# A state-space layer with a mixture of experts on one core: who writes the taps, where the imaginary parts land, how the sums are read back, and the order of the steps

## The chip, the core and the metric

The kernel runs on one core of a Trainium2 chip. The core has a matrix engine (TensorE, in the profile PE, with its weight loads apart as PEld), a vector engine (VectorE, DVE), a scalar engine (ScalarE, ACT), a general engine (GpSimd, POOL) and a queue engine (SyncE, SP), and 16 DMA engines that move data between device memory and the on-chip memories: SBUF (128 partitions) and PSUM, into which PE writes. Each engine works through its own instructions in order and waits on semaphores for the others. SP and ACT can both issue plain DMAs; POOL issues the indirect ones (scatters by a list of rows).

The metric is the device time of one execution in microseconds. Before the change: 341.56 us, the median of three runs (341.54 to 342.92).

## What is computed

All in float32, for x of shape (2, 2048, 128). It is a layer norm, a diagonal state-space layer (S4D) with a gated linear unit and two residuals, then a second layer norm and a mixture of 14 routed experts (the best two of each token) and 2 shared ones. Cut to what matters:

```python
# first half, x2 = layernorm(x)
u  = swapaxes(x2 @ in_W.T + in_b, 1, 2)
dt = exp(log_dt);  A = -exp(log_A_real) + 1j * A_imag;  dtA = A * dt[:, None]
K  = exp(dtA[:, :, None] * arange(L))
k  = 2 * einsum('hn,hnl->hl', Cc * (exp(dtA) - 1) / A, K).real
y  = causal_convolution(u, k) + u * D_skip[:, None]        # by FFT in the reference
z  = einsum('oh,bhl->bol', glu_W, gelu(y)) + glu_b
a, g = split(z);  x = x + (swap(a * sigmoid(g)) @ out_W.T + out_b + x2)
# second half, xf = layernorm(x) as 4096 rows
gates = softmax(xf @ router_w);  the two best, made to sum to 1
expert(e) = silu((xf * rsqrt(mean(xf**2)) * rms[e]) @ W1[e]) @ W2[e]
x = x + sum over the two best of gate * expert(e) + both shared experts
```

## The kernel before

**Modes and powers.** The 4096 complex modes are laid out as 128 partitions by 32. DVE computes A (line 272: the real part from an exponential, the imaginary part by a copy of the tile `aim`, line 274, which SP loaded, line 129), then the powers Z and, by doubling, PW (`double`). While it does so, X (the input, 32 blocks of 128 tokens) arrives in eight loads, the even ones issued by SP, the odd ones by ACT (line 134); PE turns the blocks and ACT copies them into XT, which shares its memory with the later tile Y.

**Taps and Toeplitz tiles.** For each of four groups g, `taps(g)` has PE multiply powers into a PSUM tile, ACT copy four strips of it into the tile `kk`, and SP write `kk` to a table in device memory, `kp` (line 403). `toeplitz(n)` for n = 2g and 2g + 1 then has SP load shifted views of that table, four loads each (line 418): those are the Toeplitz matrices with which PE convolves inside a chunk of 128 tokens (`inside`). Those of n = 5 and 6 go into XT's memory (shown as Y<-kp). `turned(g)` has PE turn the powers and ACT copy them to VT, for the sums over a chunk (`chunk_sums`). DVE combines chunk sums into states (`turns`, `scan`), PE applies them (yps<-PW,ST, in two halves of 256 matmuls), ACT takes the gelu, DVE transposes into Y.

An engine wrapped in `Ordered` (line 94) keeps its instructions in the order in which the program names them: ACT, PE and POOL from line 228, DVE from line 353, SP from the step early2; all but POOL are released after the last tile. Elsewhere the framework's scheduler orders them.

**Units, shared experts and steps.** The tokens are 8 blocks of 512. `Unit` u0 to u4 take blocks 0, 1-2, 3-4, 5-6 and 7 through the gated unit, the projection, the residual, the layer norm, the router and the choice of two experts. Its steps by engine: gate, value, project, turn, logits, count on PE; tanh, biased, rows, turned, copies, exps on ACT; gated, add, scales, unscale, choose, slots on DVE; scatter on POOL, which writes each token's row twice, to the places of its two experts in the table `xs_rows`, 8 scatters for u0 and u4, 16 for each other. `Shared` s0 to s5 do the two shared experts for one block: first (PE), silu (ACT), second (PE), add (DVE). A "scale" multiplies one expert's weights by its norm weights (ACT). early1, early2, table1 and table2 make the table of the experts' tiles. `STEPS` (line 50) is one list of 226 such steps, written out by hand; each engine takes its own from it in that order.

**Tiles.** 77 tiles of 128 rows: SP (and for odd late tiles ACT) loads the rows xg, SP copies the expert's first weights wg within SBUF, PE turns the rows and multiplies twice, ACT applies silu, DVE scales by the gate (yo), POOL scatters 128 result rows to the table `res` by the goal that travelled with each row (`goal`, line 702: 2 x 4096 rows, row 256k + 2p + a for block k, partition p and choice a).

**The tail.** `summands(j)` loads the two results of each of a block's 512 tokens (1155, all on SP, in pieces of 1 KB); `finish(j, rd)` adds the two (1160), adds X (1161) and stores (1163, SP, in pieces of 512 bytes). The shared experts of the last two blocks (LATE = 2) run here, s6 and s7; their `add` (1131) puts the PSUM tile pz into X first.

Of the kernel before, what the change touches and what calls it, by code (L numbers as in the profile page):

```python
# [18 lines left out]
P = 128  # L19
# [28 lines left out]


STEPS = """  # L50
u0.parts.0 u1.gate.0 u1.value.0 u1.biased.0 u0.gated.0 u0.project.0 u1.gate.1 u1.tanh.0
u1.value.1 u0.add.0 u1.tanh.1 u1.gated.0 u1.biased.1 u1.project.0 u0.scales u2.gate.0
u2.tanh.0 u1.gated.1 u2.gate.1 u1.project.1 u1.add.0 u2.value.1 u0.rows.0 u2.tanh.1
u2.value.0 u1.add.1 u0.turn.0 u0.unscale u0.turned.0 u2.biased.0 u2.biased.1 u0.logits.0
u0.copies.0 u1.scales u1.rows.0 u1.rows.1 u3.gate.0 u3.gate.1 u2.gated.0 u1.turn.0 u0.choose
u2.gated.1 u1.turned.0 u0.exps u2.project.0 u1.turn.1 u3.tanh.0 scale u1.turned.1 scale
scale u0.count u3.tanh.1 u2.add.0 u3.value.0 u1.logits.0 u1.logits.1 u0.slots u0.scatter
u1.copies.1 u3.biased.0 u1.unscale u2.project.1 u1.choose u3.gated.0 u1.exps s0.first.0
s0.first.1 s0.silu.0 u3.value.1 u1.count scale s0.silu.1 s0.first.2 s0.first.3 u3.project.0
u2.add.1 u1.copies.0 u1.slots u1.scatter s0.second.0 scale s0.second.1 u2.scales s0.silu.2  # L60
scale scale u3.biased.1 u3.gated.1 u2.rows.0 u3.add.0 u3.project.1 u2.turn.0 s0.second.2
u2.rows.1 u3.add.1 u2.turn.1 u2.unscale u2.turned.0 scale s0.silu.3 u2.turned.1 u3.scales
u2.copies.0 u2.logits.0 u2.copies.1 u2.logits.1 s0.second.3 scale u3.rows.0 u2.choose
s1.first.0 u3.rows.1 u3.turn.0 s1.first.1 s1.first.2 u2.count u3.turned.0 s1.silu.0 u2.exps
u2.slots u2.scatter u3.turn.1 s1.silu.1 u3.turned.1 u3.logits.0 u3.copies.0 s1.first.3
s1.silu.3 s1.second.0 u4.gate.0 s1.silu.2 u4.tanh.0 s0.add u3.logits.1 s1.second.1
s1.second.2 u3.unscale s1.second.3 u3.copies.1 u4.value.0 u3.choose u4.biased.0 u3.exps
s2.first.0 s2.first.1 u4.gated.0 s2.silu.0 s2.first.2 s1.add u4.project.0 s2.second.0
s2.silu.1 u4.add.0 u3.count s2.second.1 u4.scales u3.slots u3.scatter s2.silu.2 scale
s2.first.3 s2.silu.3 s2.second.2 s2.second.3 s3.first.0 scale s3.first.1 scale scale  # L70
s3.silu.0 s3.second.0 s3.first.2 s3.silu.1 u4.rows.0 s3.second.1 s3.silu.2 u4.turn.0
s3.first.3 u4.unscale u4.turned.0 s3.second.2 s3.silu.3 s3.second.3 s4.first.0 u4.logits.0
scale s4.first.1 scale early1 s2.add u4.choose s4.first.2 s4.silu.0 s4.second.0 s4.silu.1
s3.add u4.copies.0 s4.first.3 s4.second.1 u4.count scale s4.silu.2 s4.second.2 s4.silu.3
u4.exps s4.second.3 early2 s5.first.0 s5.first.1 s5.silu.0 s5.first.2 s5.second.0 u4.slots
u4.scatter table1 s5.silu.2 s5.silu.1 s5.first.3 s5.silu.3 s5.second.1 s5.second.2
s5.second.3 s5.add table2 s4.add
"""


# [27 lines left out]
def s4d_glu_moe_kernel(  # L108
# [112 lines left out]
    with ExitStack() as ssm:  # L221
# [160 lines left out]
        def taps(g):  # L382

            kps = pss.tile([P, P], F32, name=f"kps_{g}", tag="ps")
            for i in range(2):
                for c in range(2):
                    for a in range(4):
                        q = 8 * g + 4 * i + a
                        T.matmul(
                            kps[a * NM:a * NM + 8, :], lhsT=BC[:, c, q, :], rhs=PW[:, c, q, 0:P],  # L390
                            start=(i == 0 and c == 0), stop=False, skip_group_check=True,
                        )
            for a in range(4):
# [9 lines left out]
            Q.dma_start(out=kp, in_=kk)  # L403
            kpd[g] = kp

        def toeplitz(g):
# [691 lines left out]
    class Shared:  # L1098
# [29 lines left out]

        def add(self):
            xf = X[:, self.j * TB:(self.j + 1) * TB, :].rearrange("p k d -> p (k d)")  # L1130
            V.tensor_tensor(xf, self.pz, xf, ALU.add)

        def whole(self):
# [174 lines left out]
```

## Time and profile before

The profiled execution took 342.49 us; its span, from the first to the last instruction, is 340.8 us, and all times below count from the span's start.

| engine | busy us | share of span | instructions |
|---|---|---|---|
| PE | 267.3 | 78% | 2951 |
| PEld | 222.8 | 65% | 2951 |
| DVE | 225.3 | 66% | 787 |
| ACT | 169.6 | 50% | 434 |
| POOL | 149.5 | 44% | 249 |

| part of the execution | from, to (us) |
|---|---|
| modes, powers, states (DVE, then PE) | 4.4, 103.8 |
| gelu and transposes | 103.8, 109.5 |
| units and shared experts in the order of the list | 106.3, 207 |
| row scatters on POOL | 136.6, 217.9 |
| result scatters on POOL | 218.2, 317.4 |
| loads of results, sums, stores | 318.8, 338.9 |

Reading it: a row of a view in order of time has the start, the duration (of all its instructions together), the engine, the line, the operation, the tensors written and read, a count, and in brackets the idle time before it with what ended it; "issue" stands for an idle time that the profile can't put down to anything. L102 is the line of the helper that records ordered instructions, so tiles are told apart by name. A q after an engine's name means the engine issuing a DMA; the DMA's data move later. A row of a view by stretches has the stretch, its length, the busy time and count of PE, PEld, DVE, ACT and POOL, PE's granted clock, the DMA engines' mean busy share, and GB/s. The busy share of an engine is a mean over stages: where POOL stands at 7 tenths, the rest is the pause of 0.30 us between two scatters.

### The profile page before, as it was taken

What the parts mean: (1) busy time and instruction counts of PE and PEld (TensorE: products, weight loads), DVE (VectorE), ACT (ScalarE), POOL (GpSimd) and SP (SyncE); (2) the same over time, 40 slices, a digit from 0 to 9 for tenths busy, and PEclk for the clock granted to TensorE, in tenths of its full rate; (3) what the DMA queues carried; (4) which work ended last, traced back from release to release, by engine and by line L of the source; (5) the groups of instructions that cost most, each with busy time, mean ns of one, the idle gap of its engine ahead of it and who ended that gap; (6) DMA issues with size and microseconds to landing.
All of it is one profiled execution on the core that took longest, in us unless ns stands there. A gap on an engine that the chain in (4) does not pass through costs nothing.

```text
span 340.8 us, 8883 instructions
## 1 busy us (share of the span) xinstructions
PE 267.3 (78%) x2951; PEld 222.8 (65%) x2951; DVE 225.3 (66%) x787; ACT 169.6 (50%) x434; POOL 149.5 (44%) x249
## 2 busy tenths in 40 slices
PE   1895868756796988979989973997988978889910
PEld 1885666445695446567767752987878878777710
DVE  4999889999965598897776362452554545453093
ACT  1699594597055589779677540331332322224300
POOL 5400000000001200777777777777777777777200
PEclk9999589998997898797999997797999999999985
DMA  8300181966700991111111155656666766651398
GB/s 217 87 4 0 49 213 33 240 156 178 197 4 3 281 298 28 46 49 56 55 49 55 57 171 150 184 164 205 185 187 190 210 216 194 201 160 30 126 348 264
DMA packets 66895, 47.19 MB, mean 138 GB/s; under 512 B 7304, under 2 KB 64782, under 8 KB 66850
## 3 DMA queue, kind: packets, MB, share of 16 engines
q1 hardware_dynamic: 55906, 35.11, 36.8%
q0 software_dynamic: 4512, 8.47, 7.6%
q10 hardware_dynamic: 6432, 3.05, 3.4%
q8 instruction: 24, 0.39, 0.5%
q14 instruction: 21, 0.17, 0.2%
HBM read 24.49 MB, written 12.86 MB: 110 GB/s over the span
## 4 chain that ended last, share of the span: by engine, by line
PE 41%; DVE 27%; DMA 14%; ACT 7%; issue 5%; SPq 2%; POOL 2%; DVEq 0%; ACTq 0%; POOLq 0%
PE pz L102 12%; PE ph L102 11%; DMA xg<-xs_rows 9%; DVE t L102 6%; PE yps L102 5%; DVE PW L102 3%; PE xgt L102 3%; DMA WB<-res 2%; DMA xs_rows<-pl,si 2%; ACT pl L102 2%; POOL xs_rows L102 2%; PE pa L102 2%; PE pg L102 1%; PE pr L102 1%; DVE U L102 1%
## 5 line engine op out<-in xcount | busy, mean ns | idle before, releaser
L102 POOL DMA_INDIRECT xs_rows<-pl,si x64 | 62.1, 970 | 42.6 <-ACT pl L102 23.4
L102 POOL DMA_INDIRECT res<-yo,to x65 | 64.0, 985 | 20.1 <-issue 9.1
L102 ACT ACTIVATE hs<-ph 128x256 f32<-128x256 f32 x77 | 29.4, 384 | 78.0 <-PE ph L102 48.6
L102 DVE TENSOR_SCALAR yo<-pz,xg 128x128 f32<-128x128 f32 x77 | 27.0, 351 | 40.9 <-PE pz L102 38.2
L102 PE MATMUL pz<-WB,hs 128*128 x308 | 49.9, 285 | 1.3 <-ACT hs L102 0.8
L102 PE MATMUL ph<-xgt,wg 128*128 128x128 f32 x308 | 49.5, 285 | 0.0
L102 PEld LDWEIGHTS pz<-WB,hs 128*128 128x128 f32 x308 | 41.8, 197 | 4.0 <-ACT hs L102 2.5
L102 PEld LDWEIGHTS ph<-xgt,wg 128*128 128x128 f32 x308 | 42.7, 201 | 0.3 <-DVE xgt L102 0.3
L102 POOL MEMSET blank<- 128x130 f32 x1 | 0.2, 208 | 93.3 <-DVE Y L102 93.3
L102 PE MATMUL xgt<-ident,xg 128*128 128x128 f32 x77 | 22.6, 295 | 16.1 <-DMA xg<-xs_rows 16.0
L102 DVE COPY xgt<-xgt 128x128 f32<-128x128 f32 x77 | 21.8, 283 | 16.2 <-PE xgt L102 15.3
L102 PEld LDWEIGHTS pz<-WB,hsh 128*128 128x128 f32 x192 | 24.0, 196 | 6.7 <-ACT hsh L102 3.3
L102 PE MATMUL ph<-XRT,WB 128*128 128x512 f32 x48 | 26.0, 657 | 1.5 <-DVE sv L102 1.5
L102 PE MATMUL pz<-WB,hsh 128*128 128x128 f32 x192 | 25.5, 284 | 1.6 <-ACT hsh L102 1.6
L102 ACT ACT_TABLE_LOAD x11 | 14.1, 1283 | 20.5 <-PE yps L102 11.9
L102 PEld LDWEIGHTS xgt<-ident,xg 128*128 128x128 f32 x77 | 11.3, 147 | 19.0 <-DMA xg<-xs_rows 18.8
L102 DVE TENSOR_TENSOR t<-PW,Z 128x512 f32<-128x512 f32 (+4 forms) x26 | 20.0, 809 | 0.4
L102 ACT ACTIVATE hsh<-ph 128x512 f32<-128x512 f32 x24 | 13.8, 597 | 9.4 <-PE ph L102 9.4
L102 PE MATMUL yps<-PW,ST 32*32 32x128 f32 x512 | 15.3, 268 | 3.5 <-issue 2.6
L102 PEld LDWEIGHTS yps<-PW,ST 32*32 32x32 f32 x512 | 13.9, 104 | 4.7 <-issue 3.5
L102 PE MATMUL pt<-flip,X 128*128 128x128 f32 x64 | 10.2, 315 | 7.4 <-DMA X<-in_x_dram 7.1
L102 ACT ACTIVATE pl<-X,mr,rq_y 128x128 f32<-128x128 f32 x32 | 12.8, 480 | 3.1 <-DVE mr L102 3.1
(244 smaller groups left out, 546.7 us busy)
## 6 DMA issues: line engine op xcount, KB each, us to landing
wg<-WB SPq DMA_DIRECT2D x77, 128.0 KB
toep<-kp SPq DMA_DIRECT2D x24, 256.0 KB
WB<-res SPq DMA_DIRECT2D x7, 512.0 KB
xg<-xs_rows SPq DMA_DIRECT2D x47, 65.0 KB
Y<-kp SPq DMA_DIRECT2D x8, 256.0 KB
xg<-xs_rows ACTq DMA_DIRECT2D x30, 65.0 KB
WB<-in_w_dram SPq DMA_DIRECT2D x2, 896.0 KB
WB<-in_w_dram SPq DMA_DIRECT2D x4, 448.0 KB
```

Of the source, the lines that this page charges most:

```text
L102: return self.tc.keep_in_program_order(getattr(self.engine, name)(*args, **kwargs))
```

## The change

It has five parts. The imaginary parts are loaded straight into A, which moves to a pool that lasts, by a DMA that ACT issues ahead of its X loads; DVE's copy goes. The taps are written to `kp` by a DMA that ACT issues after its copies, not SP. The rows of `res` are numbered so that the two results of a partition's four tokens of a block lie together: the loads have pieces of 4 KB, and both loads and stores alternate between SP (even blocks) and ACT (odd ones). s6 and s7 have no add in the tail any more: after the last product, PE multiplies X's block by the identity into the same PSUM tile, and `finish` reads that tile in X's place. The list of steps has the same 226 steps in another order.

```diff
-u0.parts.0 u1.gate.0 u1.value.0 u1.biased.0 u0.gated.0 u0.project.0 u1.gate.1 u1.tanh.0
-u1.value.1 u0.add.0 u1.tanh.1 u1.gated.0 u1.biased.1 u1.project.0 u0.scales u2.gate.0
-u2.tanh.0 u1.gated.1 u2.gate.1 u1.project.1 u1.add.0 u2.value.1 u0.rows.0 u2.tanh.1
-u2.value.0 u1.add.1 u0.turn.0 u0.unscale u0.turned.0 u2.biased.0 u2.biased.1 u0.logits.0
-u0.copies.0 u1.scales u1.rows.0 u1.rows.1 u3.gate.0 u3.gate.1 u2.gated.0 u1.turn.0 u0.choose
-u2.gated.1 u1.turned.0 u0.exps u2.project.0 u1.turn.1 u3.tanh.0 scale u1.turned.1 scale
-scale u0.count u3.tanh.1 u2.add.0 u3.value.0 u1.logits.0 u1.logits.1 u0.slots u0.scatter
-u1.copies.1 u3.biased.0 u1.unscale u2.project.1 u1.choose u3.gated.0 u1.exps s0.first.0
-s0.first.1 s0.silu.0 u3.value.1 u1.count scale s0.silu.1 s0.first.2 s0.first.3 u3.project.0
-u2.add.1 u1.copies.0 u1.slots u1.scatter s0.second.0 scale s0.second.1 u2.scales s0.silu.2
...
-s2.first.0 s2.first.1 u4.gated.0 s2.silu.0 s2.first.2 s1.add u4.project.0 s2.second.0
-s2.silu.1 u4.add.0 u3.count s2.second.1 u4.scales u3.slots u3.scatter s2.silu.2 scale
...
+u0.parts.0 u1.gate.0 u1.value.0 u0.gated.0 u0.project.0 u1.tanh.0 u1.gate.1 u0.add.0
+u1.value.1 u1.biased.0 u1.biased.1 u1.tanh.1 u2.gate.0 u1.gated.0 u1.project.0 u2.tanh.0
+u2.value.0 u0.scales u0.rows.0 u1.gated.1 u1.project.1 u2.gate.1 u1.add.0 u0.turn.0
+u2.value.1 u2.biased.0 u2.tanh.1 u3.gate.1 u0.unscale u0.turned.0 u1.add.1 u2.gated.0
+u0.copies.0 u0.logits.0 u1.scales u2.biased.1 u0.choose u1.rows.0 u2.project.0 u1.turn.0
+u1.rows.1 u0.exps u2.add.0 u1.copies.1 scale u3.gate.0 u0.count u0.slots u0.scatter
+u1.turned.0 scale u1.copies.0 u3.value.0 u1.turn.1 u1.unscale u1.turned.1 u2.gated.1 scale
+u1.logits.0 u1.logits.1 scale u2.project.1 u3.tanh.0 u3.biased.0 u1.choose u3.tanh.1 u1.exps
+u1.count u2.add.1 s0.first.0 s0.first.1 s0.silu.0 u1.slots u1.scatter u3.gated.0 s0.first.2
...
+s2.second.0 scale u3.choose s2.first.3 u4.gated.0 s2.silu.1 u4.project.0 scale s2.second.1
+s2.silu.2 s2.second.2 scale s1.add s2.silu.3 scale scale u3.exps s2.second.3 u3.count
+u4.add.0 u3.copies.0 u4.scales u3.slots s3.first.0 s2.add s3.first.1 s3.silu.0 u4.rows.0
+s3.first.2 s3.silu.1 s3.silu.2 u3.copies.1 u3.scatter early1 s3.first.3 s3.silu.3
...
-    aim = load("aim", a_im, [P, NQ])
+    A = const.tile([P, 2, NQ], F32, name="A")
+    S.dma_start(out=A[:, 1, :], in_=a_im)
...
-        A = tmp.tile([P, 2, NQ], F32, name="A")
         V.tensor_scalar(A[:, 0, :], ed[:, 0, :], -1.0, None, ALU.mult)
-        V.tensor_copy(A[:, 1, :], aim)
...
             kp = dram.tile([P, 2 * P], F32, name=f"kp_{g}")
-            Q.dma_start(out=kp, in_=kk)
+            S.dma_start(out=kp, in_=kk)
...
-    G.iota(goal, pattern=[[1, 2], [2 * P, NT]], base=0, channel_multiplier=2)
+    G.iota(
+        goal.rearrange("p a (j i) -> p a j i", i=TB),
+        pattern=[[1, 2], [2 * TB * P, NB], [2, TB]], base=0, channel_multiplier=2 * TB,
+    )
...
-        def second(self, n):
+        def residuals(self):
+            return X[:, self.j * TB:(self.j + 1) * TB, :].rearrange("p k d -> p (k d)")
+
+        def second(self, n, last=False):
...
-                    start=(n == 0 and k == 0), stop=(n == 3), skip_group_check=True,
+                    start=(n == 0 and k == 0), stop=(n == 3 and not last), skip_group_check=True,
                 )
+            if last:
+
+                T.matmul(
+                    self.pz, lhsT=ident, rhs=self.residuals(), start=False, stop=True,
+                    skip_group_check=True,
+                )
...
             for n in (2, 3):
-                self.second(n)
-            yield
-            self.add()
+                self.second(n, last=n == 3)
             yield
...
-        rd = rd.rearrange("p a b -> p (a b)").rearrange("p (i b) -> p i b", i=TB)
-        rv = res.rearrange("(i p a) d -> p i (a d)", a=2, p=P)
-        Q.dma_start(out=rd, in_=rv[:, j * TB:(j + 1) * TB, :])
-        return rd
-
-    def finish(j, rd):
+        rd = rd.rearrange("p a b -> p (a b)")
+        rv = res.rearrange("(j p r) d -> p j (r d)", r=2 * TB, p=P)
+        (S if j % 2 else Q).dma_start(out=rd, in_=rv[:, j])
+        return rd.rearrange("p (i b) -> p i b", i=TB)
+
+    def finish(j, rd, rest):
         ot = rd[:, :, :P]
         V.tensor_tensor(ot, ot, rd[:, :, P:], ALU.add)
-        V.tensor_tensor(ot, ot, X[:, j * TB:(j + 1) * TB, :], ALU.add)
+        V.tensor_tensor(ot, ot, rest, ALU.add)
         ov = out.rearrange("b (i p) d -> p (b i) d", p=P)
-        Q.dma_start(out=ov[:, j * TB:(j + 1) * TB, :], in_=ot)
+        (S if j % 2 else Q).dma_start(out=ov[:, j * TB:(j + 1) * TB, :], in_=ot)
...
-            finish(k, rds[k])
+            rest = X[:, k * TB:(k + 1) * TB, :]
+            if k >= NB - LATE:
+                rest = steps[f"s{k}"].pz.rearrange("p (i d) -> p i d", i=TB)
+            finish(k, rds[k], rest)
```

More of the change, by code (lines that the diff above doesn't have):

```diff
@@ L57 @@
-scale u0.count u3.tanh.1 u2.add.0 u3.value.0 u1.logits.0 u1.logits.1 u0.slots u0.scatter
-u1.copies.1 u3.biased.0 u1.unscale u2.project.1 u1.choose u3.gated.0 u1.exps s0.first.0
-s0.first.1 s0.silu.0 u3.value.1 u1.count scale s0.silu.1 s0.first.2 s0.first.3 u3.project.0
-u2.add.1 u1.copies.0 u1.slots u1.scatter s0.second.0 scale s0.second.1 u2.scales s0.silu.2
-scale scale u3.biased.1 u3.gated.1 u2.rows.0 u3.add.0 u3.project.1 u2.turn.0 s0.second.2
-u2.rows.1 u3.add.1 u2.turn.1 u2.unscale u2.turned.0 scale s0.silu.3 u2.turned.1 u3.scales
@@ L63 @@
[L63 to L67, printed above, removed]
-s2.first.0 s2.first.1 u4.gated.0 s2.silu.0 s2.first.2 s1.add u4.project.0 s2.second.0
@@ L69 @@
-s2.silu.1 u4.add.0 u3.count s2.second.1 u4.scales u3.slots u3.scatter s2.silu.2 scale
[L70 to L74, printed above, removed]
@@ L75 @@
-u4.exps s4.second.3 early2 s5.first.0 s5.first.1 s5.silu.0 s5.first.2 s5.second.0 u4.slots
-u4.scatter table1 s5.silu.2 s5.silu.1 s5.first.3 s5.silu.3 s5.second.1 s5.second.2
-s5.second.3 s5.add table2 s4.add
+u0.parts.0 u1.gate.0 u1.value.0 u0.gated.0 u0.project.0 u1.tanh.0 u1.gate.1 u0.add.0
+u1.value.1 u1.biased.0 u1.biased.1 u1.tanh.1 u2.gate.0 u1.gated.0 u1.project.0 u2.tanh.0
+u2.value.0 u0.scales u0.rows.0 u1.gated.1 u1.project.1 u2.gate.1 u1.add.0 u0.turn.0
+u2.value.1 u2.biased.0 u2.tanh.1 u3.gate.1 u0.unscale u0.turned.0 u1.add.1 u2.gated.0
@@ new lines @@
+u0.copies.0 u0.logits.0 u1.scales u2.biased.1 u0.choose u1.rows.0 u2.project.0 u1.turn.0
[3 more added lines that the diff above has]
+u1.count u2.add.1 s0.first.0 s0.first.1 s0.silu.0 u1.slots u1.scatter u3.gated.0 s0.first.2
+s0.silu.2 u3.value.1 s0.silu.1 u2.scales u3.biased.1 s0.second.0 u2.rows.0 s0.first.3
@@ new lines @@
+s0.silu.3 scale u3.gated.1 u3.project.0 u3.add.0 u3.project.1 u2.turn.0 u3.add.1 u2.rows.1
+s0.second.1 u2.turn.1 scale s0.second.2 u2.turned.0 scale u2.turned.1 u2.logits.0
+u2.logits.1 u2.copies.0 s0.second.3 u3.scales u3.rows.0 s1.first.0 s1.first.1 u2.unscale
+u3.turn.0 u3.rows.1 s1.silu.1 u2.choose s1.first.2 u2.count u3.turn.1 s1.silu.0 s1.second.0
+u2.exps s0.add u2.copies.1 u2.slots u2.scatter u3.turned.0 u4.gate.0 s1.silu.2 s1.second.1
+u3.logits.0 s1.first.3 s1.second.2 u3.turned.1 u3.unscale s1.silu.3 u4.value.0 s1.second.3
@@ new lines @@
+u3.logits.1 u4.tanh.0 u4.biased.0 s2.first.0 s2.silu.0 s2.first.1 scale s2.first.2
+s2.second.0 scale u3.choose s2.first.3 u4.gated.0 s2.silu.1 u4.project.0 scale s2.second.1
+s2.silu.2 s2.second.2 scale s1.add s2.silu.3 scale scale u3.exps s2.second.3 u3.count
+u4.add.0 u3.copies.0 u4.scales u3.slots s3.first.0 s2.add s3.first.1 s3.silu.0 u4.rows.0
+s3.first.2 s3.silu.1 s3.silu.2 u3.copies.1 u3.scatter early1 s3.first.3 s3.silu.3
+s3.second.0 u4.turn.0 u4.turned.0 u4.unscale s3.second.1 s3.second.2 s3.second.3 s3.add
@@ L78 @@
+s4.first.0 scale s4.silu.0 u4.logits.0 s4.first.1 scale scale s4.silu.1 u4.choose s4.first.2
+s4.silu.2 s4.second.0 s4.first.3 u4.count s4.second.1 s4.silu.3 u4.exps u4.copies.0 early2
+s4.second.2 s4.second.3 u4.slots u4.scatter s5.first.0 s5.silu.0 s5.first.1 s5.first.2
+s5.second.0 s5.silu.1 s5.second.1 s5.silu.2 s5.first.3 s5.silu.3 s5.second.2 table1 table2
+s5.second.3 s4.add s5.add
 """
@@ L1125, in second @@
                     self.pz[:, ks], lhsT=hs[:, ks], rhs=w[:, HID + f:HID + f + P],
-                    start=(n == 0 and k == 0), stop=(n == 3), skip_group_check=True,
+                    start=(n == 0 and k == 0), stop=(n == 3 and not last), skip_group_check=True,
[4 more added lines that the diff above has]
+                    skip_group_check=True,
                 )
         def add(self):
-            xf = X[:, self.j * TB:(self.j + 1) * TB, :].rearrange("p k d -> p (k d)")
+            xf = self.residuals()
             V.tensor_tensor(xf, self.pz, xf, ALU.add)
```

## The prediction

> **What bounds the kernel now.** I read the page's 40 slices first, then each engine in order of time, then short stretches.
>
> ```profile
> POOL 5400000000001200777777777777777777777200
> DMA  8300181966700991111111155656666766651398
> ...
> 136.60 1.19 POOL L102 DMA_INDIRECT xs_rows<-pl,si  x1 [23.44 <-ACT pl L102]
> 138.10 0.96 POOL L102 DMA_INDIRECT xs_rows<-pl,si  x1 [0.31 <-issue]
> ...
> 281.62 0.99 POOL L102 DMA_INDIRECT res<-yo,to  x1 [0.55 <-DVE yo L102]
> ...
> 316.43 0.98 POOL L102 DMA_INDIRECT res<-yo,to  x1 [0.30 <-issue]
> ```
>
> The first line is POOL's busy share by slice, a flat 7 through the middle. In order of time POOL issues 64 row scatters and 77 result scatters from 136.60 to 317.41, one each 1.27 or 1.29 us with 0.30 between; one pause, at 281.62, is longer (0.55). So the middle is one queue of 181 us. The chain of waits names PE and ACT there, but work that ends before POOL asks for it sets nothing. Two things count: when the first scatter starts, and whether POOL ever runs dry.
>
> Ahead of 136.60 the path is DVE from 4.38 to 84.55 (modes, powers, scans), then PE's end states, the gelu, and DVE and PE on unit u0.
>
> ```profile
> 64.55 0.69 SPq L403 DMA_DIRECT2D kp<-kk  x1
> 69.51 2.02 SPq L418 DMA_DIRECT2D toep<-kp  x4
> 71.57 5.17 SPq L418 DMA_DIRECT2D Y<-kp  x4
> 76.84 0.80 SPq L403 DMA_DIRECT2D kp<-kk  x1
> ...
> 88.44 3.70 PE L102 MATMUL yps<-PW,ST 32*32 32x128 f32 x128 [0.60 <-issue]
> 94.09 0.63 PE L102 MATMUL yps<-PW,ST 32*32 32x128 f32 x14 [1.96 <-issue]
> ...
> 96.54 1.71 PE L102 MATMUL yps<-PW,ST 32*32 32x128 f32 x53
> ```
>
> SP's queue: taps 2 left ScalarE at 62.05 and taps 3 at 67.88, but SP issues them at 64.55 and 76.84, being busy with the Toeplitz loads in between. PE: 0.60 and 1.96 us idle with no wait that the profile knows ("issue"), on the path, since DVE's states were there (84.55).
>
> The tail, by stretches of 1 us (DVE and ACT busy, clock, DMA share, GB/s in the last columns):
>
> ```profile
> 322.00:323.00 1.00, 1.00 (x12) 1.00 (x11) 0.00 (x0) 0.44 (x1) 0.00 (x0) 1.00 1.08 377
> 327.00:328.00 1.00, 0.00 (x0) 0.00 (x0) 1.00 (x2) 0.00 (x0) 0.00 (x0) 1.00 1.09 348
> 337.00:338.00 1.00, 0.00 (x0) 0.00 (x0) 0.00 (x0) 0.00 (x0) 0.00 (x0) 0.50 1.15 345
> ```
>
> From 321.0 to 338.9 the DMA engines never rest. DVE, also full from 323.02, ends at 335.04; the last stores still drain for 3.8 us. The transfers set the end.
>
> **The change, part by part.** Durations are from the profiled execution (span 340.8).
>
> *Imaginary parts in place.* The copy goes; it held DVE from 5.33 to 5.45, on the path: **−0.12**. The load (0.42 on SP) moves ahead of ACT's four X loads: those come 0.47 later, and ACT, which waits 3.41 us for PE before 9.18, covers that. SP's X loads and the thirteen small ones behind them come 0.47 earlier; PE starts at 7.10 on them, but DVE is the path, so 0. A is used first at 8.23, late enough for a load issued near 0.8 (prm, issued by 1.70, landed by 4.38).
>
> *Taps by ScalarE.* Four issues leave SP and enter ACT between the kk copies and the VT copies. An ACT issue of a similar load is 0.34 to 0.35 (xg), SP's of these taps 0.33 to 0.80. Behind it on ACT stand the VT copies, for which PE waits. g=0 is on the path: kk ends 38.06, issue to 38.45, VT copy 0.59 to 39.04; PE needs that PSUM buffer at 39.17, after its second batch. Covered by 0.13, so 0; at 0.80 it would cost 0.35. For g=1 to 3 DVE, full from 48 to 94.3, covers it.
>
> What it gives back: taps 2 start at 62.1, taps 3 at 67.9. SP now stands idle 4.27 before 69.51 and 3.96 before 81.60 until taps have landed; most of that goes. The Toeplitz traffic, which now ends at about 91.9 (stretches of 2 us: share 1.12 at 88 to 90, 0.01 at 92 to 94), would end near 85.5: 4.19 MB of g=4 to 7 from 68.3, where the share now drops to 0.28, at about 245 GB/s (206 to 298 from 84 to 92).
>
> Why that matters: PE's unexplained idles come after 127, 128 and 128 matmuls with weight loads (ended 82.64, 88.44, 94.09), and the page's queue called instruction has 24 packets of 16 KB. I read them as code arriving late behind data. Once the DMA is quiet, PE runs 256 from 96.54 to 103.80 without a stop. With the traffic gone by 86, the second idle goes; the code for the first is asked for while data still flow. Without the second, the later half's states start at 94.58, not 96.54; without both, at 94.32, since DVE's last states end at 94.28; so −2.22 is the cap. The other bound: denser traffic at 71 to 83 may lengthen the idle before 82.64 from 1.19 to the longest seen, 4.59; PE has 1.27 to spare there (83.28 against 84.55), so 2.1 late, less 1.96 saved: +0.1. I take **−1.96**, the idle whose cover of traffic is gone longest.
>
> [...]
>
> *Another step list.* It has the same 226 steps. Ahead of u0.slots, DVE has one step fewer: u2.gated.1 (130.80 in the old order).
>
> ```profile
> 130.80 0.68 DVE L102 SCALAR_TENSOR_TENSOR y<-th,av 128x512 f32<-128x512 f32 x1
> 131.40 0.68 DVE L102 TENSOR_TENSOR X<-po,X 128x512 f32<-128x512 f32 x1
> ...
> 133.19 0.27 DVE L102 TENSOR_TENSOR_SCAN run<-going,pm 128x70 f32<-128x70 f32 x1
> ...
> 135.49 0.17 DVE L102 COPY pl<-goal 128x8 int32<-128x8 int32 x1
> ```
>
> DVE is without a gap from 115.25 to 135.66, so the step's 0.60 comes off. PE and ACT keep up: in the new order u0's XRT copy ends near 124.2 and its logits near 125.6, two us before DVE's choose. **−0.60**. Bounds: 0, if another wait fills it; −1.4, if POOL's 0.94 between DVE's last write (135.66) and 136.60 was a wait for the ACT copy that ended 136.45, u1.copies.1, which now stands before u0.slots.
>
> Does POOL starve? The units' first scatters come at 146.95, 167.42, 187.81 and 208.04; the slots end at 145.98, 164.55, 180.59 and 198.92. POOL asks 0.6 earlier now. u1 loses the same DVE step and a 0.50 wait for PE: ready 144.9, due 146.3. u2 gains s0.add (0.6) after it lost 1.1: about 164, due 166.8. u3.count has four more matmul steps ahead (s2.first.3, s2.second.1 to 3, some 3.6 us): slots by 184.2, its second copy, now behind s3.silu.2, by about 185; due 187.2. u4 has four fewer. No stall: 0.
>
> *Tail.* Loads are 8 of 512 KB in 1 KB pieces, then in 4 KB; stores stay 8 of 256 KB in 512-byte pieces. Per engine of 16, a 512-byte piece took 23.7 ns (stores alone, 345.5 GB/s), a 1 KB piece 43.2 (loads alone, 379). That is 4.2 fixed and 19.5 per 512 bytes; so 160 for 4 KB, 409 GB/s. 4.19 MB in 10.25 instead of 11.07: **−0.82**. Bounds: 0, if pieces cost nothing; −2.4, where DVE takes over. The two additions of 0.60 that leave DVE do not show while transfers set the end. DVE ends by 334.3: first pair landing near 323.6, then 16 operations of 0.668 (12.02 for 18 now). With 0.63 to issue and 1.8 to land (taps: 38.13 to 39.95) that is 336.5 at the earliest. Two queues save issue time, which no one awaits. PE gets 2 x 0.86 for the residual product, from 325.4 to 327.1, before the sixth and seventh sums at 331.6. Behind ACT's four loads may stand eight silu of 0.52; held to 320.9, PE would end near 333 and DVE by 335, still ahead of the transfers.
>
> Sum: 0.12 + 1.96 + 0.60 + 0.82 = **3.50**, span 337.3. The profiled execution took 342.49 with a span of 340.8; the median of the three runs is 341.56. I carry the difference: **338.1**.
>
> **The rivals.**
>
> *The idles stay* (code has another cause, or denser traffic delays it elsewhere). For: at 92 to 94 the DMA was idle and PE still waited. Against: the counts of 128. 341.56 − 1.54 = **340.0**. Chance 0.20.
>
> *The loads do not get faster*: the memory, not the piece, sets their rate; for it, mixed traffic runs at 348 like stores alone. Against: 379 in loads alone. 341.56 − 2.68 = **338.9**. Chance 0.15. [...]
>
> *POOL starves at u3: the other side.* u3.slots moved back behind s2. If PE's clock drops (0.50 at 134.5 to 138.5) in that stretch as well, each us by which u3's slots and second copy end after 187.2 is a us of the end. It is slower than before once that exceeds 3.5 us, at 190.7 against my 185, as when 5.7 us of matmuls take twice as long. At 193, 8 us late, it ends at 341.56 − 3.5 + 5.8 = **343.9**. For: the four steps; against: the granted clock, 1.00 in each stretch from 164 to 190. Chance 0.10.
>
> **How the numbers follow.** Forecast 0.55, the rest as above. A measurement of this kernel tells 0.5%, 1.7 us, from no change. Faster: 0.55, 0.15, and half of the idles' 0.20, which lies just at the bound: 0.80. Slower: 0.07, most of the starved case; the same: the remaining 0.13. The range: from 338.1 down by 0.26 (the cap), 0.8 (POOL's wait) and about 0.9 (part of the tail's bound), 336.1; up to the idles' case with a little of another term lost, 340.6.
>
> **What would show it.** Right: kp issues on ACT at about 62.1 and 67.9, Toeplitz traffic over by 87, no idle over 0.5 us on PE between 84 and 102; first scatter near 133.9, POOL without gaps for 181 us; loads alone at about 409 GB/s. Wrong: the idles moved rather than gone, a pause over 1 us on POOL, or DMA shares below 1 in the tail.

## The result, and the profile after

Six runs of each: 337.76 us median (336.33 to 340.19) against 341.86 (341.54 to 344.22). The ratio is 0.9876, 95% interval 0.9841 to 0.9911, so the change saves 1.2%, some 4.1 us; 338.1 had been predicted. The profiled execution took 337.2 us with a span of 335.5, 5.3 shorter than before.

The page of the changed kernel, busy tenths of POOL and of the DMA engines in 40 slices:

```profile
POOL 5300000000001201777777777777777777777200
...
DMA  7400191989300990111111264656666767651398
```

POOL's flat 7 is as long as before, but starts and ends earlier. The rows in order of time say where:

```profile
77.28 0.81 PE L102 MATMUL SP<-U,VT 128*32 128x32 f32 x43 [4.59 <-issue]
...
84.04 3.24 PE L102 MATMUL yps<-PW,ST 32*32 32x128 f32 x106 [0.50 <-DVE ST L102]
88.31 4.13 PE L102 MATMUL yps<-PW,ST 32*32 32x128 f32 x142 [1.02 <-issue]
...
94.25 7.23 PE L102 MATMUL yps<-PW,ST 32*32 32x128 f32 x256
...
102.57 4.62 DVE L102 STREAM_TRANSPOSE Y<-YC 128x1024 f32<-128x1024 f32 x4 [3.83 <-ACT YC L102]
111.75 0.69 DVE L102 TENSOR_TENSOR X<-po,X 128x512 f32<-128x512 f32 x1 [1.60 <-PE po L102]
...
129.09 0.27 DVE L102 TENSOR_TENSOR_SCAN run<-going,pm 128x70 f32<-128x70 f32 x1
...
131.39 0.17 DVE L102 COPY pl<-goal 128x8 int32<-128x8 int32 x1
132.50 1.19 POOL L102 DMA_INDIRECT xs_rows<-pl,si  x1 [21.58 <-ACT XRT L102]
...
312.24 0.98 POOL L102 DMA_INDIRECT res<-yo,to  x1 [0.30 <-issue]
```

PE stops for code at 77.28 as long as before (4.59; a 16 KB load on the instruction queue landed at 75.86, 1.42 ahead of the stop's end). The 1.19 before 82.64, which had time to spare, is gone, and in the first half's products it stops once (1.02) where it had stopped twice (0.60 and 1.96). Y starts 2.33 earlier, u0's residual sum 3.50, u0's slots and the first scatter 4.10. From there POOL takes 180.72 us against 180.81.

In both kernels PE waits for DVE's states before it goes on with the first half. Before the change the row was this:

```profile
84.59 3.24 PE L102 MATMUL yps<-PW,ST 32*32 32x128 f32 x106 [0.96 <-DVE ST L102]
```

So what PE does ahead of that row is covered by DVE, and the row is a mark on the path. The steps of the path, as differences between marks of the two profiles:

| stretch | before | after | difference | predicted |
|---|---|---|---|---|
| start to PE's products with DVE's states of the first half | 84.59 | 84.04 | −0.55 | −0.12 |
| to its products with the states of the second half | 11.95 | 10.21 | −1.74 | −1.96 |
| to the first transpose of Y | 8.36 | 8.32 | −0.04 | 0 |
| to u0.add | 10.35 | 9.18 | −1.17 | 0 |
| to the first scatter | 21.35 | 20.75 | −0.60 | −0.60 |
| to the end of the last scatter | 180.81 | 180.72 | −0.09 | 0 |
| to the end of the span | 23.39 | 22.28 | −1.11 | −0.82 |
| sum | 340.80 | 335.50 | −5.30 | −3.50 |

The tail of the changed kernel in order of time:

```profile
314.63 1.35 ACTq L1164 DMA_DIRECT2D WB<-res  x3
...
321.92 0.41 ACTq L1172 DMA_DIRECT2D out_dram<-WB  x1
322.43 1.58 ACT L1118 ACTIVATE hsh<-ph 128x512 f32<-128x512 f32 x3 [12.05 <-DMA WB<-res]
...
331.07 0.69 DVE L1170 TENSOR_TENSOR rd<-rd,pz 128x512 f32<-128x512 f32 x1 [1.67 <-PE pz L1135]
331.79 0.39 ACTq L1172 DMA_DIRECT2D out_dram<-rd  x1
```

s7's silus stand on ACT behind the store of block 1, which waits for its sums. So PE's last product is late, DVE's last sum waits 1.67 for it, and the last store waits behind that sum. The loads are faster than the 409 GB/s forecast. The rates of 311 to 336 in slices of 0.625 us:

```profile
GB/s 1 0 1 0 1 0 0 138 125 341 419 419 420 419 419 419 420 419 419 419 420 393 321 321 311 342 347 343 347 348 343 346 345 285 102 288 68 0 0 0
```

Loads alone run at 419 to 420, stores as before at 342 to 348. The 102 near the end is the wait for the last sum.

### The profile page after: what moved, and what is told of

It is laid out like the page before. It is cut to its first block, busy times and chain, and to the rows that moved or that the text cites. A ratio compares the mean times of both kernels' runs of the same rounds, so it can differ in the third digit from the quotient of the medians.

```text
span 335.5 us, 8902 instructions
## 1 busy us (share of the span) xinstructions
PE 267.0 (80%) x2955; PEld 222.8 (66%) x2955; DVE 224.0 (67%) x784; ACT 168.8 (50%) x434; POOL 148.1 (44%) x249
## 4 chain that ended last, share of the span: by engine, by line
DVE 29%; PE 29%; DMA 19%; POOL 8%; issue 8%; ACT 5%; SPq 2%; POOLq 0%; ACTq 0%; DVEq 0%
DMA xg<-xs_rows 11%; PE pz L102 7%; PE ph L102 7%; DVE t L102 6%; POOL xs_rows L102 6%; PE yps L102 5%; DVE PW L102 3%; DMA xs_rows<-pl,si 3%; PE xgt L102 3%; DMA WB<-res 2%; POOL res L102 2%; DVE st_b L102 2%; DMA X<-in_x_dram 2%; PE pz L1129 1%; DVE U L102 1%
## 5 line engine op out<-in xcount | busy, mean ns | idle before, releaser
L102 PE MATMUL pz<-WB,hsh 128*128 128x128 f32 x192 | 24.7, 277 | 1.7 <-DVE sv L102 1.4
L102 PE MATMUL ph<-XRT,WB 128*128 128x512 f32 x48 | 24.4, 627 | 0.3 <-ACT hsh L102 0.3
```

What stands on the lines that cost most here:

```text
L102: return self.tc.keep_in_program_order(getattr(self.engine, name)(*args, **kwargs))
```

## The experiments

Four kernels each undo one part of the changed kernel. All four ran on one chip, where the kernel before took 343.41 us (25 runs).

**The old list.**

```diff
 STEPS = """
-u0.parts.0 u1.gate.0 u1.value.0 u0.gated.0 u0.project.0 u1.tanh.0 u1.gate.1 u0.add.0
+u0.parts.0 u1.gate.0 u1.value.0 u1.biased.0 u0.gated.0 u0.project.0 u1.gate.1 u1.tanh.0
...
```

> The changed kernel with one part undone: the step list of before. In the changed kernel's trace (span 335.5) the residual of unit 0 (u0.add) starts at 111.75, DVE's slot block of u0 at 129.09, POOL's first scatter at 132.50. The prediction's theory: the list is worth the 0.60 of u2.gated.1's operation ahead of u0.slots and nothing else; u0.add stays at 111.75 give or take 0.3, the slots start at 129.7, the first scatter at 133.1, span 336.1. Rival: the further 1.17 by which u0.add came early (PE's granted clock was back at 109.8 after 3.8 us at half, before after 6.5 us) comes from the list's new order of PE's work: then u0.add falls back to 112.9, the first scatter to 134.3, span 337.3. Second rival: the list is worth nothing, since other work takes the place on DVE: 132.5, span 335.5.

Measured: 339.86 us (4 runs), ratio to before 0.9891 (0.9812 to 0.9971). In the profiled execution, the longest of the four (343.29), u0.add is at 115.41, the first scatter at 136.73, the span 341.6. Every expectation of a mark missed, because the start of this execution was already 3.7 us late by 70 us (PE waited 2.1 us in sum for its first Toeplitz loads, in instructions that the list doesn't touch). The stretch tells: from u0.add to the first scatter 21.32, against 20.75 with the new list. In the kernel before it is 21.35. In the twelve profiles of this document with the new list it is 20.71 to 20.76 ten times, and 21.00 and 21.11 in two of the third group. So the list is worth 0.60, as predicted. The rival, that the early u0.add came from the list, falls: from Y to u0.add the old list took 8.82, less than the changed kernel's 9.18.

**Taps by SyncE again.**

```diff
-            S.dma_start(out=kp, in_=kk)
+            Q.dma_start(out=kp, in_=kk)
```

> The changed kernel with one part undone: the four kp writes issued by SyncE again, behind the Toeplitz loads of the group before. The prediction's theory (late Toeplitz traffic delays PE's supply of instructions): DMA traffic runs to about 91 instead of 86.4, PE stops again for 0.5 to 0.7 us near 88 and for about 2 us near 94, the half-1 products start at 96.0 instead of 94.25, the first scatter is at 134.2 to 134.5, span 337.3. Rival (the stops come at fixed counts of PE's instructions whatever the traffic; the changed kernel still has one of 1.02): half 1 stays at 94.25 within 0.3, span 335.5. Third: if the early return of PE's clock, worth 1.17, follows from the missing stop near 94, it goes too: first scatter at 135.6, span 338.6.

Measured: 341.01 us (10 runs), ratio 0.9935 (0.9894 to 0.9977). Toeplitz traffic goes on to 92.3. PE in order of time:

```profile
84.14 7.00 PE L102 MATMUL yps<-PW,ST 32*32 32x128 f32 x234 [1.32 <-DVE ST L102]
93.09 0.63 PE L102 MATMUL yps<-PW,ST 32*32 32x128 f32 x14 [1.96 <-issue]
```

The 1.96 is back to the digit, after the same count of products; the 0.60 isn't. From the 83 chunk sums to Y it takes 32.87, as before (33.03); the four kernels so far in which ScalarE issues take 30.57, 30.79, 31.87 and 32.09. The first scatter, 135.50, is where the third case had it, with PE's clock at half for 6.8 us again. From the first tap product (kps) to the 83 chunk sums ahead of PE's long stop it takes 37.44, as before (37.32), where three kernels with ScalarE's issues take 37.84, 37.85 and 37.89 (the old list, which waited for its Toeplitz loads, 41.50): the VT copies do wait behind the issues. PE waits for VT (0.33 to 1.14 us a time) in all eleven profiles with ScalarE's issue and in none of the other three. In the changed kernel that half microsecond is cover and not path, since PE then waits 0.50 for DVE all the same (84.04).

**The old tail.** All of `second`, `whole`, `summands`, `finish` and `goal` as before, at its core:

```diff
-        (S if j % 2 else Q).dma_start(out=rd, in_=rv[:, j])
+        Q.dma_start(out=rd, in_=rv[:, j * TB:(j + 1) * TB, :])
...
-                self.second(n, last=n == 3)
+                self.second(n)
+            yield
+            self.add()
```

> The changed kernel with the tail of before: 1 KB pieces, all loads and stores on SyncE, DVE adding the shared experts' last two blocks. All up to the last scatter is the changed kernel's. The prediction's theory: the loads alone run at about 379 GB/s instead of 421, and the time from the end of POOL's last scatter to the end of the span is 23.4 instead of 22.28; last scatter ends at 313.2, span 336.6. Rival: the tail's parts cancel (the faster loads gave back what ScalarE's late silus cost): tail 22.3, span 335.5. It also tells how much the start and the middle differ between two executions of the same instructions: the first scatter should be at 132.5; where it is not, that difference is chance and not an edit.

Measured: 340.75 us (10 runs), ratio 0.9922 (0.9889 to 0.9954), span 339.4; the end of the last scatter to the end of the span 23.39, the same as before. That is the 1.1, as expected. Its first scatter came at 134.09, not at 132.50, by the same instructions: 1.59 of the marks is chance.

**The imaginary parts by way of a copy.**

```diff
-    A = const.tile([P, 2, NQ], F32, name="A")
-    S.dma_start(out=A[:, 1, :], in_=a_im)
+    aim = load("aim", a_im, [P, NQ])
...
+        A = tmp.tile([P, 2, NQ], F32, name="A")
+        V.tensor_copy(A[:, 1, :], aim)
```

> The changed kernel with the imaginary parts loaded by SyncE into a tile of their own and copied by DVE. The prediction's theory: one DVE copy of 0.12 us comes back ahead of the powers, all later marks move by 0.12 (first scatter 132.6, span 335.6). Rival: what gained was the start, not the copy: ScalarE's X loads no longer follow behind that load, the log tables land later, DVE's first operation is at 4.38 again instead of 3.86, the powers end at 35.0 instead of 34.4, and the first scatter is at 133.1, span 336.1. Third: the powers' 0.5 is hidden, since PE's Toeplitz products are bound by something else: half 1 at 94.25, span 335.5.

Measured: 340.02 us (10 runs), ratio 0.9905 (0.9868 to 0.9941). DVE's first operation is at 4.38 again, as the rival had it; in all kernels with the new load it lies between 3.42 and 4.12. The first tap product, 34.62, is as before (34.55), but kernels with the new load have it at 33.94, 34.52, 34.11 and 34.59 on the first chips. So the part gives the start 0.3 to 1.0 and the first tap product 0 to 0.7, on the mean 0.3; the ratios can't tell it from nothing.

Where the rest goes can be read on ScalarE. It computes the sines (`s`) that DVE needs for the powers, first in the kernel before, then in the changed one:

```profile
13.54 0.72 ACT L102 ACTIVATE s<-rr 128x256 f32<-128x256 f32 x2 [0.77 <-DVE rr L290]
```

```profile
12.97 0.72 ACT L102 ACTIVATE s<-rr 128x256 f32<-128x256 f32 x2
```

In both profiles with the old load ScalarE waits there for DVE (0.77, 0.58). In all twelve with the new load it waits for nothing: it comes straight from its own copies of the turned X, for which PE waits on X's loads. PE's first product on X is at 7.10 and 7.36 with the old load and between 7.25 and 9.41 with the new one (7.55 to 8.00 on the first chips), and in eight of the twelve DVE then waits 0.30 to 2.04 us for the sines. So with the new load X's loads come onto the path there, as far as two profiles against twelve can tell.

The second group asked for the cause of the stops. It and the third ran on other chips, where the kernel before takes 418.6 and 417.54 us. The scatters of the kernels profiled there take, first to last, 250 to 254 us in place of 181. Marks ahead of the scatters and in the tail can still be read.

**More traffic.**

```diff
+        for u in range(8):
+            more = dram.tile([P, 4, P], F32, name=f"more_{u}")
...
+            Q.dma_start(out=more, in_=src)
         for g in (2, 3):
             chunk_sums(g)
```

> The changed kernel with eight further loads of 256 KB behind the last Toeplitz load on SyncE, from memory to memory, whose data nobody reads (work added, none taken away). The trace shows each 16 KB of instructions as a transfer of its own on an instruction queue: 5.25 to 6 us apart while Toeplitz data is under way, 3.5 to 3.75 once it is over; 128 products of the half stages take 3.7 us. The prediction's theory (code arrives late behind the data): traffic goes on to about 93 to 95, the code loads after 86 stay 5 to 6 us apart until then, PE stops about 2 us at each, half 1 and the first scatter come 2 to 4 us later than in the changed kernel run beside it, and span grows as much. Rival (the stops belong to fixed places in PE's instructions, the traffic is no part): code loads 3.7 us apart from 86 on, stops of 1.0 to 1.2, first scatter as in the changed kernel.

**Half the traffic.**

```diff
-                toeplitz(n)
+                if n < 4:
+                    toeplitz(n)
+                else:
+                    toep[n] = toep[3]
```

> The changed kernel without the Toeplitz loads of groups 4 to 7: their products read the tile of group 3 instead, so this part of the output is another, and 16 of 32 loads (4 MB) are not made. The prediction's theory: Toeplitz traffic is over by about 66, PE's code loads are then 3.7 us apart or as far apart as PE needs them, the stop of 4.59 before 77.28 and the 1.02 before 88.31 shrink below 0.5 each, and the scan of half 0 starts some 4 us earlier; first scatter 127 to 130. Rival (fixed places): stops of 3.2 to 5.4 and of 1.0 to 2.0 as in all kernels so far, first scatter 132.5 to 135. Middle case: the 4.59 is another wait (for a bank of PSUM or the scan) and stays, the 1.02 goes: first scatter about 131.5 to 134.

PE's idle times and the DMA share from 60 to 100 us (slices of 1 us), first with more traffic, then with half:

```profile
78.38 0.60 PE L102 MATMUL SP<-U,VT 128*32 128x32 f32 x45 [4.33 <-issue]
89.27 5.36 PE L102 MATMUL yps<-PW,ST 32*32 32x128 f32 x128 [1.94 <-issue]
97.11 0.63 PE L102 MATMUL yps<-PW,ST 32*32 32x128 f32 x14 [2.49 <-issue]
```

```profile
DMA  9767999968978999999979987999997999989882
```

```profile
72.84 0.60 PE L102 MATMUL SP<-U,VT 128*32 128x32 f32 x45 [1.03 <-issue]
76.80 3.26 PE L102 MATMUL yps<-toep,U 128*32 128x128 f32 x64 [2.40 <-DVE d L102]
81.68 0.42 PE L102 MATMUL yps<-PW,ST 32*32 32x128 f32 x8 [1.62 <-DVE ST L102]
83.42 8.64 PE L102 MATMUL yps<-PW,ST 32*32 32x128 f32 x248 [1.32 <-DVE ST L102]
```

```profile
DMA  8789999400000000000000000000000000000000
```

More traffic takes 415.61 us (10 runs) and half the traffic 410.78 (4 runs), against 410.95 for the changed kernel beside them. With more traffic the code loads after 86 us come 7.6 and 4.7 apart, PE stops 1.94 and 2.49 in the halves, and the first scatter is at 139.27, against 135.69 in the changed kernel and 136.28 in the kernel with silus first beside it. With half the traffic, over at 67.5, the 4.59 shrinks to 1.03 and in the halves PE never stops for code. The rival of fixed places falls. One part of the theory missed. The first scatter (133.31) is 2.38 earlier than in the repeat below. Of this, 1.28 arises ahead of the first tap product, which the edit doesn't touch, and 1.99 from there to the chunk sums; 1.12 is lost again to PE's clock (6.8 us at half against 3.4). From the chunk sums to Y it takes 31.27 against 31.47: PE now waits 5.34 for DVE's scan instead, so the long stop near 77 lies beside that scan and costs next to nothing.

The code itself can be seen on its way. In the DMA view of the kernel before, 91.5 to 92.0 us, a 16 KB load on the instruction queue stands in the stream:

```profile
q8 instruction: 1, 0.02, 14.1%
```

Such loads come at 75.0, 80.3, 85.8 and 91.5 before (steps of 0.25 us), then at 95.3 and 99.0: 5.3 to 5.8 apart under data, 3.7 to 3.8 once it is over, which is what 128 products take (3.70). In the changed kernel they come at 80.0, 85.8, 89.3, 93.0. One of these loads takes 0.92 to 1.43 us, under data or not, so the delay lies ahead of it; whether the load waits in its queue or is asked for late, no view shows.

These loads can be tied to the stops one by one, by the times of their packets in the traces. From 70 to 104 us the fourteen profiles of this document have 36 stops of PE over 0.4 us that end by "issue", and each ends 1.22 to 1.59 us after a 16 KB load has landed. The 1.96 of the kernel before ends at 94.09; its load ran from 91.70 to 92.82, as the data ended. That is why PE still waited at 92 to 94 while the DMA engines were idle, the row that spoke for the rival.

**The changed kernel once more, and its silus first.**

```diff
         for _ in steps[f"s{j}"].whole():
-            next(ends)
+            pass
```

> The changed kernel once more, unchanged, for the spread of its marks: kernels with the same instructions up to a mark put it up to 4 us apart (first scatter 132.50 and 134.09). If the marks of PE's stops at code loads and of its granted clock are chance from execution to execution, they differ here too: stops of 0.6 to 2.3 us between the start of half 0 and the end of half 1, half-clock time 3.3 or 6.5 us, first scatter anywhere from 132.5 to 135, tail 22.0 to 22.6. If they are fixed by the instructions, all come again within 0.3.

> The changed kernel with all of the last two shared blocks (their first products, silus, second products) issued before the first finish of the tail, so that on ScalarE the eight silus stand behind the four loads alone and no longer behind the stores of blocks 1 and 3. In the changed kernel ScalarE's last silus waited 12.05 us behind the store of block 1 until 322.43, PE ended at 331.0, and DVE's last add waited 1.67 us for PE. Theory (the new wait in the tail costs what DVE waited, since the transfers end when the last store does): PE is done before 325, DVE's last add waits for nothing from PE, the last store is issued 1.2 to 1.7 us earlier, and the time from the end of the last scatter to the end of the span falls from 22.28 (mean of the four kernels with this tail: 22.3) to 20.6 to 21.3. Rival (the tail is bound by the 6 MB of transfers, whose data rate decides alone): 22.3 within 0.3, since DVE's wait was cover for transfers still under way.

The repeat: PE stops 5.58, 0.90 and 0.27, first scatter 135.69, half-clock time 3.4 us, tail 22.96; 410.95 us (6 runs). The stops vary, as the first case of the expectation had it. The kernel with silus first lets the last two shared blocks run to their end before the first `finish`: 410.74 us (6 runs), no difference. Its dip near the end of the transfers is gone and DVE's last sum waits for nothing:

```profile
403.04 0.68 DVE L1170 TENSOR_TENSOR rd<-rd,pz 128x512 f32<-128x512 f32 x1
```

Its tail is 21.81, which looks like 1.15 gained. But ACT's first load was issued 2.38 after the last scatter in the repeat and 1.44 here; counted from that issue it is 20.37 against 20.58. The rival is nearer: the transfers decide.

**Piece or queue.** The third group has two kernels that part the tail's two changes, a repeat, and a version meant to beat both (silus first, and POOL issues the taps).

```diff
-        rv = res.rearrange("(j p r) d -> p j (r d)", r=2 * TB, p=P)
-        (S if j % 2 else Q).dma_start(out=rd, in_=rv[:, j])
+        rv = res.rearrange("(i p a) d -> p i (a d)", a=2, p=P)
+        (S if j % 2 else Q).dma_start(out=rd, in_=rv[:, j * TB:(j + 1) * TB, :])
```

> The changed kernel with the rows of the result in their old order (1 KB pieces in the tail's loads) on its two queues. If the size of the pieces makes the rate: loads alone at 375 to 385 GB/s, 8 loads of 512 KB in 11.0 instead of 9.9 us, tail 1.0 longer (23.2 to 23.8). If the second queue makes it: 415 to 425 GB/s and a tail as the changed kernel's, 22.0 to 23.0.

```diff
-        (S if j % 2 else Q).dma_start(out=rd, in_=rv[:, j])
+        Q.dma_start(out=rd, in_=rv[:, j])
```

> The changed kernel with all eight 4 KB loads on SyncE, the stores on two queues as they are. If the size of the pieces makes the rate: 405 to 425 GB/s and the loads over as early as in the changed kernel, tail 22.0 to 23.0, or shorter by up to 0.7, since ScalarE's silus no longer stand behind four loads. If the second queue makes it: 375 to 385 GB/s, tail 23.2 to 23.8.

> The changed kernel once more, beside the others of this call: the spread of its marks, and the reference for the two kernels with other tails. Tail 22.0 to 23.0 from the end of the last scatter, loads alone 415 to 425 GB/s; first scatter 132.5 to 136.

The DMA rates of the last 24 us (slices of 0.6 us), first 1 KB pieces on two queues, then 4 KB on one:

```profile
GB/s 1 0 0 0 0 43 46 340 384 381 314 367 358 355 357 347 348 348 352 346 345 350 350 350 348 341 356 344 347 345 346 343 348 345 343 347 254 1 0 0
```

```profile
GB/s 14 1 27 1 0 0 0 14 143 307 294 389 396 348 382 423 416 403 423 416 430 403 430 363 342 394 387 335 343 346 349 342 345 348 344 343 282 5 0 0
```

The issue of the loads came 1.4 to 3.2 us after the last scatter, so the tail is counted from the first issue:

| kernel | pieces, queues for loads | first issue to end (us) |
|---|---|---|
| before | 1 KB, one | 21.97 |
| old tail | 1 KB, one | 21.97 |
| 1 KB on two queues | 1 KB, two | 21.99 |
| changed, eight profiles with its tail | 4 KB, two | 20.52 to 21.21, mean 20.74 |
| silus first | 4 KB, two | 20.37 |
| silus first, taps by POOL (below) | 4 KB, two | 20.63 |
| 4 KB on one queue | 4 KB, one | 20.24 |

The pieces make the whole gain, the second queue for loads none of it. The repeat's tail from the last scatter, 23.70, is outside what was expected, by its late issue alone (3.18).

```diff
-            S.dma_start(out=kp, in_=kk)
+            G.dma_start(out=kp, in_=kk)
...
-            next(ends)
+            pass
```

> A version that could beat both: the changed kernel with the last two shared blocks issued before the tail's first finish (as in silu_first) and with the four kp writes issued by POOL, which has nothing to do between 10 and 100 us. Theory: the tail is 0.8 to 1.2 shorter than the changed kernel's beside it (21.2 to 21.8 from the end of the last scatter), and ScalarE's VT copies no longer wait 0.33 to 0.63 behind an issue: from the first tap product to the 83 chunk sums ahead of the stop near 77, 37.84 us in the changed kernel and 37.3 to 37.4 where SyncE issues, it is 37.4 again; together 1.2 to 1.6 us, ratio to the changed kernel beside it about 0.996. Rival: POOL's way to issue takes longer than ScalarE's (its scatters take 0.96 us each where ScalarE's issue takes 0.35), the taps are in memory 1 us later, the Toeplitz loads of each group follow as much later, and PE waits for the first ones (0.5 to 1.5 before the first Toeplitz products): same time as the changed kernel or slower by 1.

Measured: 411.12 us (6 runs) against 409.96 for the changed kernel beside it (6 runs), 411.76 with 1 KB pieces and 409.93 with one queue: no version here is shown to be faster than the changed kernel. Its tail from the first issue, 20.63, lies among those of the changed kernel. PE no longer waits for VT copies in its profile, but stops 0.43 for code near 71 and reaches the chunk sums after 37.98, not 37.4; it doesn't wait for Toeplitz loads, as the rival had it. Whether POOL's issue is better than ScalarE's stays open.

## Why the prediction was right, and where not

**Imaginary parts, −0.12, came as −0.55 in the profile, by another way.** I had moved the loads of X by 0.47 and stopped there. The log tables, DVE's first input, land 0.52 earlier once X's loads leave later; that they share the DMA engines is argued, not tested. And "ACT covers that" failed: the 3.41 us that were to cover X's later loads are a wait for PE, which waits for those loads, and the wait grew with them (4.93 in the changed kernel). Behind it stand the sines, which the pair of profiles has just in time and eight other kernels too late. DVE's states of the first half end at 84.54 before and at 84.30 with the old load; with the new one, on the same chips, at 83.98, 84.18, 84.08 and 84.66. On the mean the part is worth 0.1 to 0.3, and the 0.55 of the pair is luck.

**Taps, −1.96: the mechanism right, −1.74 in the pair, less elsewhere.** Late data traffic did delay PE's code in these runs: adding traffic lengthened the stops in the halves (1.94 and 2.49, with 0.90 in the repeat beside it), taking half away removed those and left 1.03 of the 4.59, undoing the edit brought the 1.96 back. "No idle over 0.5 us on PE" was wrong: PE stops once more, for 0.9 to 2.0 in six of nine kernels with ScalarE's issue (0.49 to 0.74 in the other three), as I read it wherever the end of the traffic falls between two code loads. So one of the signs of being wrong, idles moved rather than gone, showed in small: 1.02 in place of 0.60. How much is left of the stops at the second half is told by how long after DVE's last states PE begins its products there: 2.26 before and 1.72 with SyncE's issue, 0.53 in the changed kernel, and 0.24 to 2.11 in eight of the nine kernels with ScalarE's issue, 0.96 on the mean (4.32 with the old list). So the gain is nearer 1 us than 2, and the pair has one of the better draws. Three of the nine also had PE wait 0.55 to 2.1 us for their first Toeplitz loads, and neither kernel with SyncE's issue did; whether that is chance stays open. The cover that I gave ScalarE's issue held in the pair, by DVE, although PE reaches the chunk sums 0.40 to 0.57 later with it.

Where the DMA engines were quiet PE seldom stopped for code (with half the traffic no stop in the 248 products from 83.42, but 1.03 before 72.84), and where data flowed the stops over 0.4 us took up to 5.58. The rival in which the idles stay, 340.0 (the sum without this term), fell.

**Granted clock, not in the sum: −1.17.** From Y to u0.add the same products took 9.18 instead of 10.35, because PE was at half clock for 3.4 us and not for 6.8: a granted clock of 0.50 from 106.19 for 3.41 us, before the change from 107.18 for 6.83, both after PE had waited 2.49 us for Y. Stretches of the changed kernel (clock, DMA share and GB/s are the last columns):

```profile
106.00:108.00 2.00, 1.66 (x7) 1.66 (x8) 1.20 (x2) 0.76 (x2) 0.56 (x9) 0.55 0.00 0
108.00:110.00 2.00, 2.00 (x6) 1.14 (x5) 0.65 (x1) 1.17 (x2) 1.81 (x22) 0.60 0.68 199
```

In all fourteen profiles the half-clock time after this idle stretch is either 3.4 or 6.8 us, nothing between. With 3.4 (six of them) the stretch from Y to u0.add takes 8.82 to 9.29, with 6.8 (eight) 9.68 to 10.46. Kernels with the same instructions up to there got both: the changed kernel 3.4 each of three times, with silus first and with 1 KB pieces 6.8. So this part is no gain of the change. Whether a run without the 1.96 stop gets the short one more often can't be said from these.

**List, −0.60: exact**, in the pair and when undone. The 0.94 between DVE's last write (131.56) and the first scatter (132.50) is the same as before, so the bound of −1.4 was no gain to be had.

**POOL: not starved in the pair, at times elsewhere.** Its one longer pause is 0.59, at 256.86; the other side's rival needed u3 to come 8 us late. But in the four kernels with one part undone the scatters take 182.26, 182.10, 181.92 and 181.15 us, with pauses of 0.5 to 1.6 us, most of them near 260 or 282, where the profile has POOL wait for DVE. So a sign of being wrong, a pause over 1 us on POOL, showed in three of them. I had put this term at 0, and up to 1.5 us of what is gained ahead of the scatters can go there.

**Tail, −0.82: mis-sized, −1.11.** 4 KB pieces run at 420 GB/s, not 409: at that rate 4.19 MB take 9.99 us in place of 11.07, which is 1.08 of it. My 409 came from a line through two unlike points, stores in 512-byte pieces and loads in 1 KB pieces, so that it came within 3% is partly luck. DVE was "still ahead of the transfers" only in my sum: the late silus, which I had named and held back to 320.9 at most, began at 322.43 in an execution that ended 1.8 earlier than forecast, and DVE's last sum waited 1.67 for PE while the stores ran low (the 102). With silus first that wait (0.74 in the repeat beside it) goes at a gain of 0.2 from the first issue, and at none in the last kernel of the third group, so it was mostly cover. The rival that loads don't get faster fell: 420 GB/s against 379.

The time, 337.76 against 338.1, hides that the pair of profiles differs by 5.3, not 3.5. Without the clock's 1.17 it is 4.1, the difference of the medians. That it agrees so well is partly luck: the first scatter comes at 132.50 and 134.09 by the same instructions, and the first two parts were worth less in the other kernels than in the pair.

## What to carry to other kernels

Where PE runs hundreds of small products under a dense stream of loads, count its instructions. A stop with no cause at every 128th product and weight load can be PE waiting for its code behind data: here each ended 1.22 to 1.59 us after a 16 KB load on the instruction queue had landed. To end the traffic sooner can then shorten the path (here nearer 1 us than 2), unless another engine's wait takes its place (with half the traffic PE waited 5.34 us for DVE's scan instead of for code). When a load is moved to another queue, follow the loads behind it to the engine that needs them. For loads that run alone, lengthen the pieces before adding a queue (here 1 KB pieces took 21.97 us to the end on one queue and 21.99 on two, 4 KB pieces 20.24 on one), and before giving an engine's queue DMAs, look for what that engine must still compute behind them (here silus that waited 12.05 us). Compare profiles by stretches between marks, and first see how far the same instructions spread.

## What the runs showed that was not expected

The issue of a load that waits for the last scatter comes 1.39 to 3.18 us after that scatter's end, in kernels alike there.

On the chips of the second and third groups the kernels lose some 70 us while the scatters run. In the repeat of the changed kernel PE and others wait at once, for something that the profile can't name (waits from 150 to 200 us: in total, times, longest):

```profile
DVE X L102 <- remote: 18.9, 2, 16.5
POOL xs_rows L102 <- ACT hsh L102: 18.3, 1, 18.3
```

The kernel before was not profiled on these chips but is as much slower, and the ratios of the changed kernel there, 0.9798 and 0.9811, agree with 0.9876 in sign; the cause of the waits stays open.
